# Expert-choice layers of a MetaFormer kernel: token statistics by VectorE, scales spread through DRAM, the eight largest found chunk by chunk

## The chip, the cores and the metric

The kernel runs on one core of a Trainium2 chip. The core has TensorE (PE: matrix multiplications and transposes, its weight loads are listed as PEld), VectorE (DVE), ScalarE (ACT), GpSimd (POOL) and SyncE (SP), which here only issues DMAs. Each engine works through its own instructions in order and waits on semaphores for the others. The metric is the device time of one execution in microseconds; lower is better.

## The reference, cut to what matters

A MetaFormer of four layers on an input of 4 images, 128 channels, 64 x 64 pixels. Each layer adds a token mixer and then a feed-forward part to `x`. The change concerns the feed-forward part of layers 1 and 2, which is the same code: a mixture of experts in which each of 64 experts chooses its 8 tokens out of 4096.

```
t = tokens(x)                                     # [4, 4096, 128]
n = (t - mean(t)) / sqrt(var(t) + 1e-5)           # per token, over its 128 channels
logits = einsum('bsd,ed->bse', n, gate_w) + gate_b
probs  = softmax(logits, axis=1)                  # over the 4096 tokens of an image
topv, topi = top_k(probs per expert, 8)           # 8 tokens for each expert and image
gathered = n[topi]
pooled   = einsum('bked,bke->bed', gathered, topv)
h   = gelu([pooled, 1] @ weight1[e])              # 128 -> 512
out = [h, 1] @ weight2[e]                         # 512 -> 128
t   = t + scatter_add(topi, out * topv)
```

## The kernel before, in words

`xs` holds the whole state in SBUF, [128 channels, 4 images, 4096 tokens], all in float32. `expert_choice` (line 1246) runs twice, for layers 1 and 2. It works on two pairs of images (`PAIRS`): a pair's 2 x 64 experts fill the 128 partitions of `chosen[p]`, [128, 4096]. The 4096 tokens of an image are cut into 8 chunks of 512 (`CH`, `NCH`).

Inside each `manual_schedule(engines=ORDERED)` block the instructions of PE, ACT, DVE and POOL stay in the order in which the code issues them. SP isn't in that set; its DMAs are put in order by the framework's scheduler, which also makes all waits and lets a tile's buffer be used again when its last reader is done.

Before the first block the weights of the first four groups of experts are asked for (`weights`, 8 DMAs of 1 MB, `load`, line 1316). Then the first stage (lines 1326 to 1533) does the following, in the order written at its end:

- `stat` (1337) centres one chunk by a matmul with `cent` (`moe_pd`, 128x512), squares it on ACT, and `variances` sums four squares at a time over the channels by matmuls with `ewin` into `pv`. 16 chunks make a pair. `scales` takes the square root on ACT, `inverted` the reciprocal on DVE (128x512), and `turn_scales` turns the scales so that tokens lie on partitions.
- `logits` (1383) spreads a chunk's scales over the experts by a matmul with the constant `own` (`moe_rb`), multiplies the tokens with the centred gate (`moe_pl`), copies the first to SBUF on ACT, multiplies both on DVE, and adds the bias on ACT.
- `rows` (1411) transposes a chunk of one image (four 128x128 transposes into a PSUM bank with the tag `b`, of which there are 3), copies it to one of five `xt` tiles and appends the token's scale (so that a table row has 128 + 16 numbers); a DMA on SP's queue writes it to `tables[p]` in DRAM.
- `largest` (1426) searches the 4096 logits of each expert for the eight largest (`max`, `max_index`), makes table rows of their places, and the negated maximum.
- `exponentials` and `denominators` (1441, 1447) sum the softmax on ACT, a chunk at a time.
- `ask` (1452) fetches one chosen token per expert from the table, by an indirect DMA of POOL; eight of them make a pair.
- `pool` (1462) multiplies `ident` with share and scale (`diag`) on DVE, and sums the eight gathered tokens by matmuls; a matmul with `cent` centres the sum, and a copy on DVE puts it into `pooled`.

The order: statistics of pair 0, five chunks of statistics of pair 1, logits and `largest` of pair 0, the rest of the statistics mixed with `rows` of image 0, logits of pair 1 mixed with `rows` and with exponentials of pair 0, `largest(1)`, the last `rows` and the `ask`s of pair 0, exponentials and `ask`s of pair 1, `pool(0)`, `pool(1)`.

The second stage runs the 16 groups of experts through `first`, `turn`, `second` and `hand`, with the weights coming from DRAM; the last stage multiplies each token's results back and adds them to `xs`.

Two other phases use forms that matter below: the recurrence of layer 0 measures its inputs with `bn_stats` (line 499), and the attention of layer 3 has an `inverse_root` of small VectorE operations (1853) and spreads its scales through DRAM (`spread` at 1922, `way` at 1925).

Of the kernel before, what the change touches and what calls it, by code (L numbers as in the profile page):

```python
# [17 lines left out]
F32 = mybir.dt.float32  # L18
# [1227 lines left out]
def expert_choice(net, layer):  # L1246
# [20 lines left out]
    K, ROW = 8, P + 16  # L1267
# [3 lines left out]
    with ExitStack() as ctx:  # L1271
        dram = ctx.enter_context(tc.tile_pool(name="moe_dram", bufs=1, space=bass.MemoryType.DRAM))
        tables = [dram.tile([2 * N, ROW], F32, name=f"moe_table{p}") for p in range(PAIRS)]
# [24 lines left out]
        behind = keep.tile([P, 1], F32, name="moe_behind")  # L1298
        nc.gpsimd.memset(behind[0:E], 0.0)
        nc.gpsimd.memset(behind[E:P], float(N))  # L1300
# [25 lines left out]
        with (  # L1326
# [5 lines left out]
            def bank(tag, name):  # L1332
                return ps.tile([P, CH], F32, name=f"moe_{name}", tag=tag, bufs={"a": 3, "b": 3}.get(tag, 1))

            stats = {}

            def stat(p, j):

                if j == 0:
                    stats[p] = (bank("pv", "pv"), [])  # L1340
                pv, squares = stats[p]
                pd = bank("a", "pd")
                nc.tensor.matmul(pd, net.cent, net.chunk(2 * p + j // NCH, j % NCH), start=True, stop=True)
                sq = sb.tile([P, CH], F32, name="moe_sq", tag="moe_sq", bufs=5)
                nc.scalar.activation(sq, pd, AF.Square)
                squares.append(sq)
                if j % 4 == 1 and j > 4:
                    variances(p, j // 4 - 1)

            def variances(p, r):  # L1350
                pv, squares = stats[p]
                for q in range(4):
                    nc.tensor.matmul(
                        pv[32 * q : 32 * q + 32],
                        net.ewin[:, 31 - r : 63 - r],
                        squares[4 * r + q],
                        start=r == 0,
                        stop=r == 3,
                    )

            rstds, turned = {}, {}

            def scales(p):
                variances(p, 3)
                rstd = sb.tile([P, CH], F32, name="moe_rstd", tag="moe_rstd")
                nc.scalar.activation(rstd, stats[p][0], AF.Sqrt, bias=net.eps[1e-5])
                rstds[p] = rstd

            def inverted(p):
                nc.vector.reciprocal(rstds[p], rstds[p])  # L1370

            def turn_scales(p):

                pt = bank("a", "pr")
                for k in range(4):
                    nc.tensor.transpose(pt[:, k * P : (k + 1) * P], rstds[p][:, k * P : (k + 1) * P], net.ident)
                turned[p] = sb.tile([P, 2, NCH, 4], F32, name="moe_turned", tag="moe_turned")
                nc.vector.tensor_copy(
                    turned[p].rearrange("p i (a q) k -> p k q (i a)", q=4),
                    pt.rearrange("p (k q r) -> p k q r", q=4, r=32)[:, :, :, 0:4],  # L1380
                )

            def logits(p, c):
                pb, pl = bank("b", "rb"), bank("a", "pl")
                q = c % 4
                rows = slice(32 * q, 32 * q + 32)
                nc.tensor.matmul(pb, own[rows, c // 4, :], rstds[p][rows], start=True, stop=True)
                for i in range(2):
                    nc.tensor.matmul(
                        pl[i * E : (i + 1) * E], cgate, net.chunk(2 * p + i, c), start=True, stop=True  # L1390
                    )
                lg = chosen[p][:, c * CH : (c + 1) * CH]
                nc.scalar.copy(lg, pb)
                nc.vector.tensor_mul(lg, lg, pl)
                nc.scalar.activation(lg, lg, AF.Identity, bias=gbias)

            xts = [sb.tile([P, 4, ROW], F32, name=f"moe_xt{i}", bufs=1) for i in range(5)]
            for t in xts:
                nc.gpsimd.memset(t[:, :, P:ROW], 0.0)

            own = sb.tile([P, 2, 2 * E], F32, name="moe_own", bufs=1)
            for q in range(4):
                group = slice(32 * q, 32 * q + 32)
                for r in range(2):
                    for i in range(2):
                        at = 32 * q + 2 * i + r
                        nc.gpsimd.tensor_copy(
                            own[group, r, i * E : (i + 1) * E], net.ident[group, at : at + 1].to_broadcast([32, E])
                        )

            def rows(b, c):
# [3 lines left out]
                for t in range(4):  # L1415
                    tok = slice((4 * c + t) * P, (4 * c + t + 1) * P)
                    nc.tensor.transpose(pt[:, t * P : (t + 1) * P], net.xs[:, b, tok], net.ident)
# [34 lines left out]
            def ask(p, j):  # L1452
                if j == 0:
                    asked[p] = sb.tile([P, K, ROW], F32, name="moe_asked", tag="moe_asked")
# [31 lines left out]
            for j in range(2 * NCH):  # L1486
                stat(0, j)
# [1144 lines left out]
```

## Time and profile before

| | us |
|---|---|
| median of 3 runs | 6042.37 (6040.1 to 6043.02) |
| the profiled execution's own time | 6034.38 |
| its span, first to last instruction | 6032.6 |
| first stage of `expert_choice`, layer 1 | 2461.8 to 2584.5 |
| second stage, layer 1 | 2584.5 to 2664.5 |
| first stage, layer 2 | 2934.9 to 3054.8 |
| second stage, layer 2 | 3054.8 to 3130.3 |

Over the span PE is busy 5684.2 us (94%), DVE 4380.3 (73%), ACT 3365.4 (56%), POOL 2057.2 (34%). In the first stage of layer 2 (119.9 us) PE is busy 101.0 us, ACT 72.3, DVE 44.6, at a granted TensorE clock of 0.91.

A line of the timeline gives the start and the duration in us, the engine, the line of the source, the operation, output and inputs with their shapes, how often it was merged, and in brackets how long the engine had idled before and what ended that. `SPq` is SP's queue of DMAs: its time is that of the issue, not of the transfer.

### The profile page before, as it was taken

Reading aid. Unit: us, or ns where it says so; the run is one execution under the profiler, and the core shown is the slowest. Engines: PE = TensorE matmul, PEld = TensorE weight load, DVE = VectorE, ACT = ScalarE, POOL = GpSimd, SP = SyncE. Lnnn points to the kernel's source line nnn. Section 1 sums busy time; section 2 is a strip of 40 time slices with the busy share of each in tenths; the row PEclk is TensorE's granted clock in tenths of the full one; section 3 lists DMA queues with packets and bytes.
Section 4 is the critical chain, followed back from the end, with each engine's and each line's share of the span. In section 5 each row is a group of like instructions: output and inputs, shape, how many; then the busy total and the mean of one; then the engine's idle time right before and its main releaser. Section 6 shows DMA issues by size and latency. Waiting matters only on the chain. (4 is left out here: it accounts for less than half of the span.)

```text
span 6032.6 us, 97814 instructions
## 1 busy us (share of the span) xinstructions
PE 5684.2 (94%) x39896; PEld 2250.6 (37%) x39927; DVE 4380.3 (73%) x4783; ACT 3365.4 (56%) x4213; POOL 2057.2 (34%) x2015
## 2 busy tenths in 40 slices
PE   8999999889999988879979999999999999999799
PEld 2222222346667766433333222322232223222233
DVE  6888887456767676456446888888888888888666
ACT  4444444333323322521336888888888888999421
POOL 3898897027777777200010111111111111111000
PEclk9999999989999999979989999999999999999899
DMA  6434432057777777550274666656665666666200
GB/s 215 98 74 90 89 76 47 1 150 231 217 229 217 228 221 210 167 183 0 88 266 111 133 155 146 138 130 154 146 141 128 151 148 142 133 131 131 60 25 27
DMA packets 273274, 818.39 MB, mean 136 GB/s; under 512 B 42644, under 2 KB 100392, under 8 KB 226728
## 3 DMA queue, kind: packets, MB, share of 16 engines
q0 software_dynamic: 109568, 505.75, 35.2%
q1 hardware_dynamic: 163240, 306.20, 17.5%
q8 instruction: 320, 5.24, 0.4%
q14 instruction: 146, 1.20, 0.1%
HBM read 416.71 MB, written 93.13 MB: 85 GB/s over the span
## 5 line engine op out<-in xcount | busy, mean ns | idle before, releaser
L2035 ACT ACTIVATE att_ex<-att_sc,att_shift 128x1024 f32<-128x1024 f32 x2048 | 2141.8, 1111 | 281.3 <-PE att_sc L2031 165.1
L2066 DVE TENSOR_TENSOR att_dve<-att_dve,att_ex 128x2048 f32<-128x2048 f32 x704 | 1631.5, 2317 | 154.0 <-ACT att_ex L2035 129.2
L2031 PE MATMUL att_sc<-att_q,att_k 32*128 32x512 f32 x8192 | 1280.8, 640 | 0.0
L2047 PE MATMUL att_pv<-att_ex,att_vals 128*32 128x512 f32 x8192 | 1092.2, 605 | 0.0
L998 POOL DMA_INDIRECT dcn_g<-dcn_table,dcn_idx x896 | 851.3, 950 | 354.3 <-issue 150.8
L412 DVE SCALAR_TENSOR_TENSOR inv_prod<-inv_pk,bspan,inv_seen 128x512 f32<-128x512 f32 (+1 forms) x1120 | 774.5, 743 | 141.4 <-PE inv_pk L399 141.0
L410 POOL TENSOR_TENSOR inv_prod<-inv_seen,inv_prod 128x512 f32<-128x512 f32 (+1 forms) x672 | 837.5, 1273 | 95.2 <-ACT inv_prod L409 95.2
L2064 POOL DMA_DIRECT2D att_dma<-att_ex x224 | 192.5, 859 | 1965.1 <-ACT att_ex L2035 1738.6
L409 ACT ACTIVATE inv_prod<-inv_pk,bspan 128x512 f32<-128x512 f32 (+1 forms) x672 | 436.1, 682 | 504.9 <-PE inv_pk L399 493.7
L2031 PEld LDWEIGHTS att_sc<-att_q,att_k 32*128 32x128 f32 x8192 | 423.5, 183 | 656.5 <-issue 416.8
L1006 DVE TENSOR_TENSOR dcn_g<-dcn_g,dcn_near_w 128x1024 f32<-128x1024 f32 x448 | 538.9, 1214 | 164.9 <-DMA dcn_g<-dcn_table,dcn_idx 153.4
L399 PE MATMUL inv_pk<-inv_red,wtap 32*96 32x512 f32 (+1 forms) x3584 | 512.1, 637 | 7.3 <-DVE wtap L377 7.3
L1015 PE MATMUL dcn_pt<-ident,dcn_g 128*128 128x128 f32 x3584 | 472.9, 276 | 34.0 <-ACT dcn_st L1120 16.4
L1015 PEld LDWEIGHTS dcn_pt<-ident,dcn_g 128*128 128x128 f32 x3584 | 419.1, 142 | 206.9 <-issue 116.1
L421 PE MATMUL inv_out<-inv_prod,inv_fold 96*32 96x512 f32 (+1 forms) x3584 | 478.6, 606 | 8.5 <-DVE xs L429 8.5
L2047 PEld LDWEIGHTS att_pv<-att_ex,att_vals 128*32 128x32 f32 x8192 | 161.8, 108 | 752.2 <-issue 727.0
L399 PEld LDWEIGHTS inv_pk<-inv_red,wtap 32*96 32x96 f32 (+1 forms) x3584 | 131.9, 171 | 386.2 <-DVE inv_prod L412 362.5
L1034 ACT ACTIVATE dcn_fold<-dcn_pf,dcn_turn 128x256 f32<-128x256 f32 x128 | 60.2, 473 | 366.0 <-PE dcn_pf L1030 366.0
L1120 ACT COPY dcn_st<-dcn_pt 128x512 f32<-128x512 f32 x224 | 129.9, 580 | 241.0 <-PE dcn_pt L1015 241.0
L1127 PE MATMUL dcn_out<-dcn_st,dcn_wk 128*128 128x512 f32 x448 | 236.0, 609 | 25.0 <-DVE xs L1135 23.1
L2536 PE MATMUL top_po<-top_xg,top_we 128*128 128x512 f32 x512 | 233.3, 599 | 0.0
L1054 DVE TENSOR_TENSOR dcn_square<-dcn_hx,dcn_by 128x512 f32<-128x512 f32 x192 | 130.0, 677 | 115.4 <-PE dcn_by L1040 75.5
(442 smaller groups left out, 5358.1 us busy)
## 6 DMA issues: line engine op xcount, KB each, us to landing
att_dma<-att_ex POOLq DMA_DIRECT2D x224, 1024.0 KB, 7.0
inv_seen<-inv_image SPq DMA_DIRECT2D x256, 266.0 KB, 9.1
moe_w<-in_L_ffn_weight SPq DMA_DIRECT2D x64, 1024.0 KB, 14.2
att_dma<-att_ex SPq DMA_DIRECT2D x32, 1024.0 KB, 9.0
att_dve<-att_dma POOLq DMA_DIRECT2D x32, 1024.0 KB
moe_table<-moe_xt SPq DMA_DIRECT2D x64, 288.0 KB, 2.8
dcn_table<-dcn_xt SPq DMA_DIRECT2D x32, 512.0 KB, 4.8
dcn_g<-dcn_table,dcn_idx POOLq DMA_INDIRECT x896, 3.7
```

What stands on the lines that cost most here:

```text
L399: nc.tensor.matmul(pk[0:m], wtap[half][rg, i, blk], red[rg, h * CH : (h + 1) * CH], start=True, stop=True)
L409: nc.scalar.activation(prod[0:m, h], pk[0:m], AF.Identity, bias=by)
L410: nc.gpsimd.tensor_mul(of, view, of)
L412: nc.vector.scalar_tensor_tensor(out=of, in0=as_shape(pk[0:m], of), scalar=by, in1=view, op0=ALU.add, op1=ALU.mult)
L421: nc.tensor.matmul(po[CR * blk : CR * (blk + 1), h, :], fold[0:m], prod[0:m, h, :], start=unit == 0, stop=unit == UNITS - 1,)
L998: nc.gpsimd.indirect_dma_start(out=g[:, t, :], out_offset=None, in_=rows, in_offset=bass.IndirectOffsetOnAxis(ap=idx[:, Q4 * c + i + t, k ...
L1006: nc.vector.tensor_mul(near, near, by)
L1015: nc.tensor.matmul(pt[0][:, (i + t) * P : (i + t + 1) * P], near[:, t, q, :], net.ident, is_transpose=True, start=i + t + q == 0, stop=i + ...
L2031: nc.tensor.matmul(pes[h // 2][:, h % 2, :], ks[r, t * P : (t + 1) * P], q[r], start=True, stop=True)
L2035: nc.scalar.activation(ex[:, 2 * two : 2 * two + 2, :], pes[two], AF.Exp, bias=shifts[g][:, two : two + 1],)
L2047: nc.tensor.matmul(block["pv"][r], vals[:, t, r], ex[:, h, :], start=t == 0, stop=t == NT - 1)
L2066: nc.vector.tensor_add(block[who], block[who], ex)
```

## The change

Nothing outside `expert_choice` is touched. A table row now is the token alone (128 numbers), and token 4p + t of a chunk lies on partition p (the transposes take every fourth token), so that a partition writes four rows in one piece. `rows` no longer needs the scales and so comes first. The token's statistics are taken by DVE from the transposed chunk in PSUM: four `bn_stats` of 128 numbers each, which give count, mean and spread of the even and the odd channels (`halves`); `variance` joins the two halves. `scales` takes square root and reciprocal of all 64 values per partition of a pair, transposes them, writes them to DRAM (`spread`), and `way` reads 512 scales back for each chunk, repeated on 64 partitions for each image; three `by` buffers hold them. `logits` multiplies with that tile.

`largest_of` finds the eight largest and their places in each chunk as it comes; `largest` searches the 64 candidates of the eight chunks and then looks up the eight places by eight comparisons with a counter (`order`). The scales of the fetched tokens are no longer fetched: `pool` measures the fetched rows again, and takes the inverse root by `inverse_root` on DVE. The `b` banks are 4 instead of 3, the `diag` buffers 3 instead of 4. The order of the stage is new.

```diff
-            for j in range(2 * NCH):
-                stat(0, j)
-            scales(0)
-            inverted(0)
-            for j in range(5):
-                stat(1, j)
-            turn_scales(0)
...
+            def variance(halves, out, apart):
+                nc.vector.tensor_sub(apart, halves[..., 1], halves[..., 4])
+                nc.vector.tensor_mul(apart, apart, apart)
+                nc.vector.tensor_add(out, halves[..., 2], halves[..., 5])
+                nc.vector.scalar_tensor_tensor(
+                    out=out, in0=apart, scalar=P / 4.0, in1=out, op0=ALU.mult, op1=ALU.add
+                )
+                nc.vector.tensor_scalar(out, out, 1.0 / P, 1e-5, op0=ALU.mult, op1=ALU.add)
...
+            def rows(b, c):
+                p, i = divmod(b, 2)
+                pt = bank("b", "pt")
+                for t in range(4):
+                    nc.tensor.transpose(pt[:, t * P : (t + 1) * P], net.chunk(b, c)[:, t:CH:4], net.ident)
+                xt = xts[(b * NCH + c) % len(xts)]
+                nc.scalar.copy(xt, pt.rearrange("p (t d) -> p t d", d=P))
+                for t in range(4):
+                    nc.vector.bn_stats(halves[p][:, i, c, t, :], pt[:, t * P : (t + 1) * P])
+                first = i * N + c * CH
+                nc.sync.dma_start(tables[p][first : first + CH, :].rearrange("(p t) r -> p t r", t=4), xt)
...
             def scales(p):
...
+                variance(halves[p].rearrange("p i c t h -> p (i c t) h"), var, apart)
+                nc.scalar.activation(var, var, AF.Sqrt)
+                nc.vector.reciprocal(var, var)
                 pt = bank("a", "pr")
+                nc.tensor.transpose(pt[0 : 2 * NCH * 4, 0:P], var, net.ident)
+                lines = sb.tile([2 * NCH * 4, P], F32, name="moe_lines", tag="moe_lines", bufs=1)
+                nc.vector.tensor_copy(lines, pt[0 : 2 * NCH * 4, 0:P])
+                nc.sync.dma_start(spread[p].rearrange("i c (t q) -> (i c t) q", q=P), lines)
+                for c in range(2):
+                    way(p, c)
+
+            def way(p, c):
+                by = ways[p, c] = sb.tile([P, CH], F32, name="moe_by", tag="moe_by", bufs=3)
+                for i in range(2):
+                    nc.sync.dma_start(by[i * E : (i + 1) * E], spread[p][i, c : c + 1, :].to_broadcast([E, CH]))
...
+                by = ways.pop((p, c)).rearrange("p (t q) -> p q t", t=4)
+                nc.vector.tensor_mul(lg.rearrange("p (q t) -> p q t", t=4), by, pl.rearrange("p (q t) -> p q t", t=4))
                 nc.scalar.activation(lg, lg, AF.Identity, bias=gbias)
+                if c + 2 < NCH:
+                    way(p, c + 2)
...
+            def largest_of(p, c):
+                lg = chosen[p][:, c * CH : (c + 1) * CH]
+                nc.vector.max(out=peaks[p][:, c, :], in_=lg)
+                nc.vector.max_index(out=spots[p][:, c, :], in_max=peaks[p][:, c, :], in_values=lg)
...
+                nc.vector.tensor_scalar_mul(negs[p], top[:, 0:1], -1.0)
+                nc.vector.max_index(out=place, in_max=top, in_values=flat)
...
+                for j in range(K):
+                    nc.vector.scalar_tensor_tensor(
+                        out=found[:, j, :],
+                        in0=order,
+                        scalar=at[:, j : j + 1],
+                        in1=known.rearrange("p c k -> p (c k)"),
+                        op0=ALU.is_equal,
+                        op1=ALU.mult,
+                    )
+                nc.vector.tensor_reduce(row, found, AX.X, ALU.add)
...
+                for j in range(K):
+                    nc.vector.bn_stats(own[:, j, :], asked[p][:, j, :])
+                var, root, spare = (small[:, n] for n in range(3))
+                variance(own, var, spare)
+                inverse_root(root, var, spare, small[:, 3].bitcast(I32))
+                nc.vector.tensor_mul(shares[p], shares[p], root)
...
+            for b in range(2):
+                for c in range(NCH):
+                    rows(b, c)
             scales(0)
+            left = [(b, c) for b in range(2, B) for c in range(NCH)]
+            for _ in range(6):
+                rows(*left.pop(0))
             for c in range(NCH):
                 logits(0, c)
+                for _ in range(2):
+                    if left:
+                        rows(*left.pop(0))
+                        if not left:
+                            scales(1)
+                if c > 0:
+                    largest_of(0, c - 1)
+            largest_of(0, NCH - 1)
             largest(0)
             for c in range(NCH):
                 logits(1, c)
+                ask(0, c)
+                exponentials(0, c)
+                if c > 0:
+                    largest_of(1, c - 1)
             denominators(0)
+            largest_of(1, NCH - 1)
             largest(1)
+            for c in range(K):
+                ask(1, c)
                 exponentials(1, c)
             denominators(1)
             pool(0)
```

More of the change, by code (lines that the diff above doesn't have):

```diff
@@ L1332, in bank @@
             def bank(tag, name):
[L1333 to L1361, printed above, removed]
-            def scales(p):
[L1364 to L1367, printed above, removed]
@@ L1369, in inverted @@
-            def inverted(p):
-                nc.vector.reciprocal(rstds[p], rstds[p])
-            def turn_scales(p):
-                pt = bank("a", "pr")
[L1375 to L1381, printed above, removed]
+                return ps.tile([P, CH], F32, name=f"moe_{name}", tag=tag, bufs={"a": 3, "b": 4}.get(tag, 1))
@@ L1398, in expert_choice @@
[L1398 to L1409, printed above, removed]
@@ L1453, in ask @@
                 if j == 0:
[L1454 removed]
+                    asked[p] = sb.tile([P, K, P], F32, name="moe_asked", tag="moe_asked")
                 nc.gpsimd.indirect_dma_start(
```

106 lines of the change are left out of this document (44 added, 62 removed).

## The prediction

> **What bounds the kernel now.** The table of engines on the page says only that TensorE is busy 94% of the span, an average over stages with different limits; the change touches the first stage of `expert_choice`, which runs once in layer 1 (2461.8 to 2584.5 us) and once in layer 2 (2934.9 to 3054.8 us). I read the timeline of that stage, then the DMA view of its opening, then rows of other phases that already run the operations the change adds.
>
> The timeline of layer 1 (start, duration, engine, line, operation; in brackets the idle time before it and what ended it):
>
> ```profile
> 2461.78 7.34 PE L1343 MATMUL moe_pd<-xs,cent 128*128 128x512 f32 x12 [7.15 <-PEq L1182]
> 2470.69 3.37 SPq L1322 DMA_DIRECT2D moe_w<-in_L_ffn_weight  x1
> 2483.95 3.35 DVE L1370 RECIPROCAL moe_rstd<-moe_rstd 128x512 f32<-128x512 f32 x1 [28.65 <-ACT moe_rstd L1366]
> 2491.12 0.69 DVE L1394 TENSOR_TENSOR moe_chosen<-moe_chosen,moe_pl 128x512 f32<-128x512 f32 x1 [1.70 <-PE moe_pl L1389]
> ...
> 2555.80 4.43 DVE L1428 MAX8 moe_top<-moe_chosen 128x8 f32<-128x4096 f32 x1 [0.72 <-ACT moe_chosen L1395]
> 2560.34 4.42 DVE L1431 FIND_INDEX8 moe_place<-moe_top,moe_chosen 128x8 uint32<-128x4096 f32 x1
> 2571.31 0.16 DVE L1450 TENSOR_REDUCE moe_total<-moe_sums 128x1 f32<-128x8 f32 x1 [5.82 <-ACT moe_sq L1445]
> 2571.84 2.86 DVE L1469 TENSOR_SCALAR moe_diag<-ident,moe_share,moe_asked 128x128 f32<-128x128 f32 x8
> 2584.21 0.29 DVE L1482 COPY moe_pooled<-moe_pc 128x128 f32<-128x128 f32 x1 [2.51 <-PE moe_pc L1481]
> ```
>
> TensorE with ScalarE sets the statistics (VectorE has idled 28.65 us before the first reciprocal); the logits start at 2491.1 in layer 1 and at 2961.6 in layer 2. At the end VectorE leads: `largest(1)`, then ScalarE's exponentials, then the two `pool` calls, 13.2 us from 2571.31 to 2584.5.
>
> The DMA view of 2455 to 2495, 1 us to a number:
>
> ```profile
> GB/s 231 401 397 10 0 8 25 88 225 395 372 92 145 317 401 391 356 399 414 387 383 391 391 383 385 385 389 391 387 111 23 0 0 0 0 0 0 0 0 0
> ```
>
> The queue of SP carries 8 MB of expert weights at 388 GB/s, and empties at 2484.4; the same in layer 2 until 2961.4. One weight load took SP 3.37 us to issue, so the queue is full. Before, the first `moe_table` write goes out at 2509.8, long after.
>
> From the recurrence and attention, operations like the added ones:
>
> ```profile
> 1087.70 2.59 DVE L499 BATCH_NORM_STATS2 rnn_stats<-rnn_pd 128x6 f32<-128x512 f32 x4
> ...
> 3178.39 0.19 DVE L1859 TENSOR_TENSOR att_scale<-att_scale,att_turned 128x32 f32<-128x32 f32 x1
> 3178.62 0.18 DVE L1860 TENSOR_SCALAR att_scale<-att_scale 128x32 f32<-128x32 f32 x1
> 3179.92 0.34 SPq L1922 DMA_DIRECT2D att_spread<-att_scale  x1
> 3181.39 4.82 SPq L1927 DMA_DIRECT2D att_by<-att_spread  x3
> 3184.58 0.69 DVE L1938 TENSOR_TENSOR att_k<-att_by,att_sc 128x512 f32<-128x512 f32 x1 [4.72 <-DMA att_by<-att_spread]
> ```
>
> A chain of small VectorE operations steps every 0.22 us; a spread through DRAM takes 4.7 us from its write's issue to the first use (3179.92 to 3184.58).
>
> **The change, part by part.** D is the moment when the weights have drained.
>
> *Opening.* Removed are 64 `moe_pd` and 64 `moe_pv` matmuls, 32 squares, the square roots and two 3.35 us reciprocals. Instead `rows` comes first and each row ends in a table write on SP's queue, behind the 8 MB. Only five `xt` buffers and four `b` banks exist: rows 0 to 4 are copied, rows 5 to 8 transposed and measured, then PE, ACT and DVE wait. The queue serves in order by the trace (weight loads land 14.2 us after issue, 14.9 in layer 2, about five loads of 2.7 us deep). So the first table lands at D + 2.3 (0.7 us for 256 KB at 388 GB/s, and the 1.6 that remain of the shortest landing, 2.4 us for 288 KB), row 5's copy takes 0.6, row 9's four transposes 0.6: row 9's statistics start at D + 3.5. The first matmul also waits for `moe_gate` (issued 2462.7 and 2934.3, some 2.3 to 3 us); D hides it, else 2 to 4 us. The 80 POOL memsets (0.09 us, 7 us) are needed only at `largest`.
>
> *Statistics.* Four `bn_stats` of 128 per row. The 512-wide one lasts 0.698 and steps every 0.63 (2.59 less the last, over 3); at 1.04 us per 1000 elements (the 4096-wide against 512-wide rows) 384 elements less is 0.23. Bounds: 0.14 with no fixed cost, 0.30 with no overlap (the 128x128 copy from PSUM is 0.289). I take 0.23, the same operation: 0.95 a row with its wait. [...]
>
> *VectorE from D + 3.5 to the places of pair 1.* ACT's copies (0.58 a row, the 32 of 0.2 for the scales gone) and PE's transposes (0.55; 0.75 if the step of four in their loads costs what L1560's does) stay below it. The removed `rb` matmuls (1.1 a chunk) and their ACT copies (0.58) stood on the logits' path of 2.06 a chunk, which VectorE's 2.17 to 4.1 replaces. 23 rows x 0.95 = 21.9. Two `scales` with nothing in between: five operations of 64 (1.1), square root 0.5 with its handoffs, reciprocal of 64 0.5 (128 take 0.9), transpose and copy 1.1: 3.2 x 2 = 6.4. The spread of pair 0 is hidden by six rows (5.7 against 4.7 plus 0.4 for the second half); uncovered it costs 5.1. Logits 16 x 0.65 = 10.4 (the scale tile is read with a step of 128 elements; the convolution's step of two costs nothing, 0.68), bias on ACT beside them. The eight largest of a chunk: MAX8 of 4096 is 4.43, so 0.16 fixed and 0.69 at 512; with the load (0.09) and FIND_INDEX8 1.52; x 16 = 24.3 (bounds 1.2 to 1.8), against 17.9 before, of which layer 1 exposed only the second pair's 9. `largest` on 64: two short searches, casts, eight scalar operations of 64 at 0.30 (by the 8-wide 0.23), a reduce: 4.3 x 2 = 8.6. Waits on SP: `way(0, 7)` stands behind pair 1's spread and two `way`s that need buffers of chunks 5 and 6, 2.5; in pair 1's loop a `way` is asked only two chunks ahead (3.7 round trip, 2.4 a chunk instead of 2.17), 2.0; last bias 0.3: 4.8. Sum 76.4: places of pair 1 at D + 79.9, that is 2564.3 (before 2565.4) and 3041.3 (before 3035.6).
>
> *Gathers.* `ask(0)` starts at once and is hidden. `ask(1)`: 8 x 1.25 plus 2.6 landing, done by D + 92.9; DVE reaches pool 1 at D + 97, so it is hidden.
>
> *End.* `negs` is written first, so exponentials(1) start at D + 76.0; 8 x 0.9, 0.3 and the reduce bring D + 83.6. Then the pools. Before: 7.0 and 6.3 us (layer 1: 2571.31 to 2578.3 to 2584.5), 6.3 and 6.0 with asks waited off (layer 2). Each adds eight `bn_stats` (1.8), variance (1.1), inverse root 14 x 0.21 = 2.9, one multiply 0.2 and 0.2 for three `diag` buffers instead of four: 6.2. End: D + 83.6 + 7.0 + 6.3 + 12.4 = 2593.7, +9.2 us; layer 2 D + 83.6 + 6.3 + 6.0 + 12.4 = 3069.7, +14.9.
>
> The later stage keeps its order and its 32 MB; it moves along. Its fifth weight group is issued when the first stage frees its memory (2584.24); were that address free early, 2 MB at 388 GB/s, 5.4 us a layer, would be gained; no row shows it, so I take nothing.
>
> Sum: +24 us. The profiled execution took 6034.4 and would take 6058.5; the runs shown have a median 8 us above it, 6042.4, and the forecast is **6066**.
>
> **Rivals.**
> - *Table writes don't queue behind the weights* (not slower). If DMA engines served them between the loads, statistics would begin at 2467 and 2937.5 and the 32 rows run through: 12.3 and 18.8 us earlier than the forecast, 24 - 31 = -7, 6035, no change. Landings of 14 us speak against it; it decides from 6 us a layer on, tables landing before D - 4.
> - *Cheap pieces*: `bn_stats` at 0.14 (108 x 0.09 = 9.7 a layer) and searches at 1.2 (4.8): -29, 6037, no change. The fixed cost in the rows of 512 speaks against it.
> - *The spread starves*: attention's `way` lands in 5.5 us median when the queue is used, not 3.2. Then pair 1's chunks take 3.3 and `way(0, 7)` 2 more: +9 a layer, 6084.
> - *Dear pieces*: 0.30 and 1.8: 108 x 0.07 + 4.8 = 12.4 a layer, 6091.
> - *Stage two starts early*: -11, 6055.
>
> **How the numbers follow.** Forecast 0.42, no queueing 0.14, cheap 0.12, starved spread 0.15, dear 0.12, early stage two 0.05. A measurement of this kernel tells about 0.2%, 12 us, from no change. The two cases at 6035 to 6037 give most of "same" and, where both or one meets an early stage two, of "faster": faster 0.10, same 0.19, slower 0.71. The range takes in all priced cases, with 5 us below the lowest: 6030 to 6092; the likeliest case by itself 6052 to 6080.
>
> **What would show it.** Right: `moe_table` writes issued from about 2474 and none landed before 2484; a gap of some 10 us on DVE ending near D + 3.5; first logits near D + 19 to 20; `bn_stats` 0.23 apart; pair 1's places at D + 80; about 6 us more in each pool, DVE busy through it. Wrong: tables landing before D, DVE idle in the middle of the chunk loops waiting for `moe_by`, or `moe_w` issued before the last `moe_pooled`.

## The result and the profile after

The changed kernel takes 6074.82 us (median of 5 runs, 6067.61 to 6076.99), the kernel before 6040.59 us in the same comparison (5 runs, 6037.6 to 6043.02): a ratio of 1.0057, with a 95% interval of 1.0045 to 1.0068. It is slower by 34 us; the forecast was 6066 us.

The profiled execution of the changed kernel is the one that took 6074.82 us (span 6073.0). Its phases against those of before, in us, read from the timeline. The first stage runs from the cast of `dcn_flag` (layer 1) or the end of the last addition of `conv_po` (layer 2) to the end of the last copy to `moe_pooled`; the second ends with the last addition and multiplication of `moe_ot`. (The table ahead of the prediction counts layer 1 from its first matmul, 6.6 us after the flag, and ends the second stages 1.1 us earlier, where `moe_ot` begins.)

| | before | after |
|---|---|---|
| start of the cast of `dcn_flag` | 2455.2 | 2460.8 |
| first stage, layer 1 | 129.3 | 143.4 |
| second stage, layer 1 | 81.2 | 78.6 |
| third stage and convolution | 269.2 | 268.7 |
| first stage, layer 2 | 119.9 | 139.6 |
| second stage, layer 2 | 76.6 | 77.1 |

The two first stages cost 283.0 us and not 249.2, 33.8 us more, which is nearly the whole difference of the medians. The spans of the two profiled executions differ by 40.4 us: besides the first stages, the flag comes 5.6 us later, in code that the change doesn't touch, and 1.0 us lies elsewhere.

The timeline of VectorE in layer 1 of the changed kernel (start, duration, engine, line, operation; in brackets the idle time before it and what ended it):

```profile
2476.19 4.25 DVE L1362 BATCH_NORM_STATS2 moe_halves<-moe_pt 128x6 f32<-128x128 f32 x20 [15.27 <-ACT moe_xt L1360]
2492.79 8.86 DVE L1362 BATCH_NORM_STATS2 moe_halves<-moe_pt 128x6 f32<-128x128 f32 x44 [12.36 <-ACT moe_xt L1360]
...
2511.67 1.06 DVE L1395 TENSOR_TENSOR moe_chosen<-moe_by,moe_pl 128x512 f32<-128x512 f32 x1 [0.73 <-DMA moe_by<-moe_spread]
2513.99 1.68 DVE L1362 BATCH_NORM_STATS2 moe_halves<-moe_pt 128x6 f32<-128x128 f32 x8 [1.26 <-ACT moe_xt L1360]
...
2546.99 1.03 DVE L1395 TENSOR_TENSOR moe_chosen<-moe_by,moe_pl 128x512 f32<-128x512 f32 x1 [2.25 <-DMA moe_by<-moe_spread]
...
2577.52 0.17 DVE L1436 CAST moe_idx<-moe_row 128x8 int32<-128x8 f32 x1
2580.18 0.16 DVE L1449 TENSOR_REDUCE moe_total<-moe_sums 128x1 f32<-128x8 f32 x1 [2.49 <-ACT moe_sq L1444]
...
2580.58 1.64 DVE L1478 BATCH_NORM_STATS2 moe_own<-moe_asked 128x6 f32<-128x128 f32 x8
...
2603.88 0.29 DVE L1492 COPY moe_pooled<-moe_pc 128x128 f32<-128x128 f32 x1 [2.15 <-PE moe_pc L1491]
```

VectorE now leads from the first statistic to the end. After five rows (20 statistics) it stands still for 12.36 us; in layer 2 for longer:

```profile
2980.11 8.80 DVE L1362 BATCH_NORM_STATS2 moe_halves<-moe_pt 128x6 f32<-128x128 f32 x44 [21.28 <-ACT moe_xt L1360]
```

What it waits for is a copy on ScalarE, and that waits for a table write. ScalarE's and SP's lines of the same timeline, and the DMA view of 2455 to 2495 (the last line: issues, KB each, median us from issue to landing):

```profile
2478.93 0.58 ACT L1360 COPY moe_xt<-moe_pt 128x512 f32<-128x512 f32 x1 [0.21 <-PE moe_pt L1358]
2492.18 2.45 ACT L1360 COPY moe_xt<-moe_pt 128x512 f32<-128x512 f32 x4 [12.66 <-DMA moe_table<-moe_xt]
```

```profile
2477.30 2.51 SPq L1327 DMA_DIRECT2D moe_w<-in_L_ffn_weight  x1
2479.91 20.81 SPq L1364 DMA_DIRECT2D moe_table<-moe_xt  x16
```

```profile
moe_table<-moe_xt SPq DMA_DIRECT2D x9, 256.0 KB, 10.2
```

SP issues the last of the 8 MB of weights at 2477.3, then the table writes; the one whose landing the trace shows there lands 10.2 us after its issue, where later ones of this stage take 2.0 to 3.4. The sixth copy needs the first of the five `xt` buffers back.

In the whole first stage of layer 1 (one row: start and end, length, busy time of PE, PEld, DVE, ACT and POOL with the number of instructions, granted TensorE clock, DMA share, GB/s), before and after:

```profile
2455.00:2585.00 130.00, 103.70 (x402) 45.31 (x402) 44.95 (x63) 73.70 (x168) 18.18 (x34) 0.87 0.47 149
```

```profile
2461.00:2605.00 144.00, 57.02 (x236) 36.54 (x236) 91.32 (x323) 44.62 (x89) 19.86 (x101) 0.64 0.45 155
```

The change does what it says: TensorE's busy time falls from 104 to 57 us and ScalarE's from 74 to 45, VectorE's doubles from 45 to 91. With some 52 us of idle time VectorE's stage is longer than TensorE's was. TensorE is idle more, and its granted clock in this stage was 0.64 where it had been 0.87.

### The profile page after: what moved, and what is told of

Its sections match the earlier page's. It is cut to its first block, busy times and chain, and to the rows that moved or that the text cites. A ratio compares the mean times of both kernels' runs of the same rounds, so it can differ in the third digit from the quotient of the medians.

```text
span 6073.0 us, 97689 instructions
## 1 busy us (share of the span) xinstructions
PE 5595.0 (92%) x39564; PEld 2229.2 (37%) x39595; DVE 4472.1 (74%) x5305; ACT 3307.2 (54%) x4055; POOL 2057.7 (34%) x2129
## 5 line engine op out<-in xcount | busy, mean ns | idle before, releaser
L1015 PE MATMUL dcn_pt<-ident,dcn_g 128*128 128x128 f32 x3584 | 473.6, 276 | 37.9 <-ACT dcn_st L1120 13.8
L1120 ACT COPY dcn_st<-dcn_pt 128x512 f32<-128x512 f32 x224 | 129.9, 580 | 241.9 <-PE dcn_pt L1015 241.9
```

The costliest lines, as they stand in the source:

```text
L1015: nc.tensor.matmul(pt[0][:, (i + t) * P : (i + t + 1) * P], near[:, t, q, :], net.ident, is_transpose=True, start=i + t + q == 0, stop=i + ...
```

## The experiments

The experiments ran on several chips. The kernel before took 6039 us on one and 6247 to 6263 us on the others, so times are compared only as ratios to the kernel before on the same chip, and stages by their lengths in the trace. The last column is the sum of the two first stages. Each stage length is read from one profiled execution; the two of the kernel before differ by 1.6 us in that sum.

| run | ratio to before (95%) | first stage, layer 1 | layer 2 | sum |
|---|---|---|---|---|
| before, first profile | | 129.3 | 119.9 | 249.2 |
| before, on a chip of the experiments | | 130.2 | 120.6 | 250.8 |
| the change | 1.0057 (1.0045 to 1.0068) | 143.4 | 139.6 | 283.0 |
| weights asked for late | 1.0027 (1.0017 to 1.0037) | 136.7 | 127.4 | 264.1 |
| tokens in order | 1.0035 (1.0021 to 1.0048) | 140.0 | 135.1 | 275.1 |
| no statistics in the pooling | 1.0021 (1.0012 to 1.0031) | 134.5 | 129.4 | 263.9 |
| chunks' eight alone, shared buffer | 0.9998 (0.9989 to 1.0007) | 134.0 | 121.7 | 255.7 |
| weights issued by ScalarE | 1.0011 (1.0002 to 1.0020) | 133.1 | 123.7 | 256.8 |
| rows ahead of logits | 1.0058 (1.0044 to 1.0072) | 144.2 | 139.4 | 283.6 |
| four edits | 0.9991 (0.9982 to 1.0000) | 128.1 | 117.0 | 245.1 |
| and scales in place | 0.9976 (0.9965 to 0.9987) | 120.5 | 111.8 | 232.3 |
| order, rows, scales in place | 1.0048 (1.0032 to 1.0064) | 140.9 | 136.4 | 277.3 |
| chunks' eight alone, apart | 0.9996 (0.9987 to 1.0006) | 129.9 | 121.4 | 251.3 |
| all, scales in halves | 0.9946 (0.9934 to 0.9958) | 116.0 | 106.8 | 222.8 |

**The weights late.** The theory is the prediction's first step: the table writes queue behind the weights.

```diff
-        weights = [load(g) for g in range(EARLY)]
+        weights = []
...
                 logits(1, c)
+                if c == 5:
+                    weights.extend(load(g) for g in range(EARLY))
                 ask(0, c)
```

> The changed kernel, with the four early weight groups (8 MB) asked for only after the last fetch of pair 1's scales, in the sixth chunk of pair 1, and not ahead of the stage. Theory (the table writes queue behind the weights, and through the five copy buffers hold up the statistics): the idle stretches of VectorE in the opening, 12.4 us in layer 1 and 21.3 us in layer 2 in the changed kernel's profile, go nearly whole, and the time falls by 25 to 33 us, to 6042 to 6050. Rival 1 (statistics, copies or transposes set the pace of the opening anyway): the wait is only renamed, and the time stays at 6070 to 6076. Rival 2 (8 MB in some 31 us asked for this late, behind which the gathered rows of pair 1 land late): the opening gains, and what it gains comes back at the end of the stage or in the first weight wait of stage two; 6055 to 6070.

The stages fell by 18.9 us and the ratio from 1.0057 to 1.0027 (6057 us for a kernel before of 6041): more than rival 1 allows, less than the theory, and in rival 2's range, but not by its mechanism. The reason is in SP's part of the timeline (layer 1):

```profile
2680.42 0.59 SPq L1325 DMA_DIRECT2D moe_w<-in_L_ffn_weight  x1
2684.53 11.66 SPq L1364 DMA_DIRECT2D moe_table<-moe_xt  x16
2696.24 0.45 SPq L1327 DMA_DIRECT2D moe_w<-in_L_ffn_weight  x1
```

SP's order isn't the code's: the scheduler had put three of the eight loads ahead of the first table write and the rest between the later DMAs. VectorE's lines show the two sides:

```profile
2684.53 12.95 DVE L1362 BATCH_NORM_STATS2 moe_halves<-moe_pt 128x6 f32<-128x128 f32 x64 [15.67 <-ACT moe_xt L1360]
...
2711.53 0.89 DVE L1362 BATCH_NORM_STATS2 moe_halves<-moe_pt 128x6 f32<-128x128 f32 x4 [5.68 <-ACT moe_xt L1360]
```

The 64 statistics of pair 0 run in one piece, 12.95 us; a wait of 5.68 us comes back later, behind the loads now put there. So the loads were next issued by ScalarE, whose order is fixed:

```diff
+                if c % 2 == 0:
+                    weights.append((load_first(c // 2, nc.scalar),))
+                else:
+                    weights[-1] += (load_second(c // 2, nc.scalar),)
                 if c > 0:
                     largest_of(1, c - 1)
```

> The changed kernel with the eight early weight loads issued by ScalarE, one for each chunk of pair 1, where its order is fixed (SyncE's is chosen by the scheduler, which in the run with late weights put three of the eight loads ahead of the first table write all the same). Theory (the table writes queue behind the weights): no idle stretch of VectorE over 2 us is left in the opening; against the changed kernel's 143.4 us the first stage of layer 1 is 10 to 14 us shorter, and against 139.6 us that of layer 2 is 17 to 23 us shorter; the time is 1.001 to 1.002 of the kernel before's. Rival 1 (the loads then collide with the fetches of pair 1's scales and with the gathers): half of that or less, ratio 1.003 or more. Rival 2 (the issues on ScalarE hold up the exponentials of pair 0 and with them the bias that the search waits for): the opening is free, and pair 1's chunks take 3 us and not 2.33.

The stages fell by 26.2 us, 10.3 in layer 1 and 15.9 in layer 2, and the ratio to 1.0011. From VectorE's list of waits in layer 1 (what waited, for what: us, times, longest):

```profile
DVE moe_halves L1370 <- DMA moe_b<-in_L_ffn_weight: 10.6, 1, 10.6
DVE moe_chosen L1403 <- DMA moe_by<-moe_spread: 8.8, 4, 3.4
DVE moe_halves L1370 <- ACT moe_xt L1368: 7.5, 6, 1.3
```

(The first row is the wait before the stage's first statistic, which the kernel after has too, 15.27 us long, with loads of weights ahead of the gate's DMA.) No wait for a copy is over 1.3 us: that the table writes waited behind the weights is shown, and it cost 26 us net, over three quarters of the 33.8. Whether they waited because they share SP's queue or because they share the DMA engines with the weights, this run doesn't separate, since it moves the loads in time as well. The gain is a little under what was expected, and rival 1 has a part in that: VectorE now waits longer for fetches of the scales, 8.8 us in layer 1 and 6.3 in layer 2 where the changed kernel had 3.0 and 2.9. Of the fetches of layer 1 whose landing the trace shows, two issued ahead of the first load land after 2.7 and 3.1 us, two issued behind it after 7.7 and 6.9, although the loads are on another queue. Rival 2 falls: where no fetch is late, pair 1's chunks still follow one another every 2.3 us.

**Tokens in order.** In the changed kernel the logits' multiply takes 1.02 us where the multiply before took 0.69. The scale tile is the only new operand, and it is read with a step of 128 numbers.

```diff
-                    nc.tensor.transpose(pt[:, t * P : (t + 1) * P], net.chunk(b, c)[:, t:CH:4], net.ident)
+                    nc.tensor.transpose(pt[:, t * P : (t + 1) * P], net.chunk(b, c)[:, t * P : (t + 1) * P], net.ident)
...
-                by = ways.pop((p, c)).rearrange("p (t q) -> p q t", t=4)
-                nc.vector.tensor_mul(lg.rearrange("p (q t) -> p q t", t=4), by, pl.rearrange("p (q t) -> p q t", t=4))
+                nc.vector.tensor_mul(lg, ways.pop((p, c)), pl)
```

> The changed kernel with each transpose taking 128 neighbouring tokens, as the kernel before did, so that the scales come back in token order and the logits' multiply reads them without a step (the table rows are then written in runs of 512 bytes). Theory (the step is what made the multiply 1.03 us where the kernel before had 0.69): 16 multiplies by 0.34 us less in each layer, on the engine that sets the pace: 5.4 us a layer, 11 in all, 6062 to 6066. Rival 1 (the step costs nothing, the multiply is long because its second operand comes from another place): the multiplies stay at 1.0 us and the time at 6072 to 6077. Rival 2 (runs of 512 bytes make the table writes late): the multiplies fall to 0.69 but the copies wait for the writes, 6070 to 6080.

The tile view of `moe_chosen` (duration in ns, least, median and most), the changed kernel first:

```profile
L1395 DVE TENSOR_TENSOR moe_chosen<-moe_by,moe_pl x16: 1004/1024/1058, 2511.7 to 2569.9; 128x512 f32<-128x512 f32 x16
```

```profile
L1394 DVE TENSOR_TENSOR moe_chosen<-moe_by,moe_pl x16: 667/669/689, 2738.4 to 2792.3; 128x512 f32<-128x512 f32 x16
```

The step cost 0.355 us a multiply, 5.7 us a layer. The two stages fell by 7.9 us together and the ratio by 0.0022. The rest of the 11.4 us went into idle time, most of it in layer 1, where VectorE idles 54.8 us instead of 52.5: one multiply waits 1.4 us, by the profile for a table write, and the copies of rows are waited for 1.0 us longer. The waits for fetches did not grow (2.5 us for one, where two had taken 3.0). Rival 1 falls: the operand still comes from the same place.

**No statistics in the pooling.**

```diff
-                for j in range(K):
-                    nc.vector.bn_stats(own[:, j, :], asked[p][:, j, :])
-                var, root, spare = (small[:, n] for n in range(3))
-                variance(own, var, spare)
-                inverse_root(root, var, spare, small[:, 3].bitcast(I32))
-                nc.vector.tensor_mul(shares[p], shares[p], root)
```

> The changed kernel without the statistics and the inverse root of the gathered rows: the shares go into the diagonals unscaled, so the pooled tokens lack each row's norm scale. Theory (nothing covers these operations, they stand in a row on VectorE between the reduce and the diagonals): 5.8 us in each of two poolings, 11.6 us a layer, 23 in all: 6050 to 6053. Rival (the gathered rows of pair 1 or the diagonals' banks come late anyway): only pair 0's half is won, 6061 to 6065.

The stages fell by 8.9 and 10.2 us, 19.1 together, the ratio to 1.0021. That is nearer the theory (23) than the rival (half): the operations stand in the path of both pairs, and a part returns as waits for TensorE between the two poolings (1.1 us ahead of the copy to `moe_b1t`).

**The chunks' eight alone.** The kernel before got this one part of the change.

```diff
             for c in range(NCH):
                 logits(1, c)
+                if c > 0:
+                    largest_of(1, c - 1)
```

> The kernel before with one part of the change alone: the eight largest from each chunk's eight, and the negated maximum taken first; the table rows are 136 wide and not 144, to make room. Theory (in the kernel before ScalarE sets the pace there: its copies of the last image's rows run to 2564.5 in the profile, the exponentials start at 2565.5 when VectorE has the maximum): VectorE has the maximum some 8 us sooner, but ScalarE is free only 1 us sooner, so 1 to 2 us a layer are won: 6036 to 6040. Rival 1 (VectorE's search sets the end of the stage): 7 to 8 us a layer, 6024 to 6028. Rival 2 (eight more searches a pair hold up the logits' loop): slower than before, 6042 to 6055.

The ratio is 0.9998, no difference, but the stage of layer 1 was 134.0 us. One suspect in the trace: `found` in `largest` takes a buffer that the squares of the statistics take turns in, and a square waited 2.25 us for it. So the part was tried again with `found` in a PSUM bank of its own:

```diff
-                found = sb.tile([P, CH], F32, name="moe_sq", tag="moe_sq", bufs=5)
+                found = bank("acc", "acc")
```

> The kernel before with the eight largest from each chunk's eight alone, as in the run of this part alone, but with the looked-up places in a PSUM bank of their own, and not in a buffer that the squares of pair 1's statistics take turns in: in that run a square waited 2.3 us for it, TensorE then stood still and worked at a lower granted clock (0.84 and 0.82 where the kernel before has 0.91 and 1.00). Theory (that stall ate the gain, and ScalarE sets the end as said): the stages are 1 to 2 us shorter each than in the kernel before, 250.8 us together on this chip: 247 to 249, ratio 0.9992 to 0.9998. Rival (the searches themselves delay the logits' multiplies): 252 us or more, ratio above 1.0003.

The ratio is 0.9996 and the stages take 251.3 us, 250.8 in the kernel before: the first run's 134.0 us in layer 1 are gone (129.9), and nothing is won. The buffer doesn't explain the 134.0: a square waited as long for it in layer 2, whose stage was as long as in this run (121.7 against 121.4), and in layer 1 the 4 us arise later. The eight multiplies of pair 1 start within 28.0 us there and within 24.7 here, at these granted clocks (the last column but two) in 15 us of that stretch, the shared buffer first:

```profile
2757.60:2772.60 15.00, 15.00 (x43) 6.36 (x42) 4.81 (x10) 9.43 (x25) 0.00 (x0) 0.58 0.32 94
```

```profile
2744.20:2759.20 15.00, 14.06 (x62) 6.32 (x61) 6.55 (x14) 12.21 (x32) 0.00 (x0) 0.96 0.41 122
```

The kernel before, which has no such sharing, took 24.6 us at a clock of 0.99 in its first profile and 26.6 at 0.80 in its second. So a single profile's stage can be some us longer at a lower clock; what lowered the clock, no run shows. VectorE and ScalarE at the end of layer 1's first stage:

```profile
2772.01 0.15 DVE L1443 TENSOR_SCALAR moe_neg<-moe_top 128x1 f32<-128x1 f32 x1
...
2785.39 0.16 DVE L1478 TENSOR_REDUCE moe_total<-moe_sums 128x1 f32<-128x8 f32 x1 [8.90 <-ACT moe_sq L1473]
```

```profile
2773.80 0.58 ACT L1423 COPY moe_xt<-moe_pt 128x512 f32<-128x512 f32 x1 [2.01 <-issue]
...
2779.62 0.72 ACT L1473 ACTIVATE moe_sq<-moe_chosen,moe_neg 128x512 f32<-128x512 f32 x1
```

The negated maximum is there at 2772.0, but ScalarE copies rows until 2779.6: VectorE's gain became a wait of 8.90 us. The searches of the whole tile had been hidden by ScalarE's copies.

**Rows ahead of logits.** Five times in each layer VectorE waits 1.26 us for a copy that stands behind the logits' bias on ScalarE.

```diff
-                logits(0, c)
                 for _ in range(2):
                     if left:
                         rows(*left.pop(0))
                         if not left:
                             scales(1)
+                logits(0, c)
```

> The changed kernel with the two rows of a chunk issued ahead of its logits, and not after them, in the loop of pair 0. Theory (in five chunks of each layer VectorE waits 1.26 us for a copy on ScalarE that stands behind the logits' bias): the five waits go, 6.3 us a layer, 12.6 in all; the ratio to the kernel before falls from 1.0057 to 1.0035 or so. Rival (the transposes or the bias are then late by as much): the waits go to another instruction, ratio 1.005 to 1.006.

The rival is right: 283.6 us against 283.0, ratio 1.0058. Four of the five waits are gone; in their place two fetches of scales are late and the first matmul of pair 1. From the list of waits in layer 1, rows ahead first, then the changed kernel:

```profile
DVE moe_chosen L1395 <- DMA moe_by<-moe_spread: 4.7, 2, 2.4
...
DVE moe_chosen L1395 <- PE moe_pl L1390: 1.6, 1, 1.6
```

```profile
DVE moe_chosen L1395 <- DMA moe_by<-moe_spread: 3.0, 2, 2.3
...
DVE moe_chosen L1395 <- PE moe_pl L1390: 0.2, 1, 0.2
```

and in layer 1 VectorE waits 1.0 us longer for the copies behind the table writes in the opening and 1.7 us more among the six rows.

**All together, and the fetches.** The four edits in one kernel (weights by ScalarE, tokens in order, rows ahead, and `pool` split so that pair 0's rows are measured and its diagonals made ahead of pair 1's sum, pair 1's measured while TensorE works):

```diff
-            denominators(1)
-            pool(0)
+            measure(0)
+            mix(0)
+            denominators(1)
+            measure(1)
+            finish(0)
```

> The changed kernel with these four at once: the weights issued by ScalarE, tokens in order, rows ahead of logits, and in the pooling the order changed (pair 0's rows are measured and its diagonals made ahead of pair 1's sum of exponentials, for which VectorE waited 2.5 us, and pair 1's rows are measured while TensorE works for pair 0). If the costs found are separate terms they add up: 14 + 21 (weights) + 9.5 (tokens in order, as measured) + 12 (rows) + 8 (pooling) = 64 us of the two first stages, 283 us in the changed kernel's profile and 249 in that of the kernel before: 219 to 230 us, and a ratio to the kernel before of 0.995 to 0.997. Rival (TensorE or the table writes set the pace once VectorE is quicker; the opening then waits for the transposes, and the pooling for the gathers): 235 to 250 us and a ratio of 0.998 to 1.000.

245.1 us, a gain of 37.9 of the 64 expected, ratio 0.9991: the rival's range. The first line of the list of waits in layer 1 names what came next:

```profile
DVE moe_chosen L1402 <- DMA moe_by<-moe_spread: 13.4, 6, 4.9
```

These waits are of two kinds. Before any weight load is issued, two multiplies of pair 0 wait 5.6 us together, where the fetches shown land 3.1 to 3.5 us after their issue: they are asked for late, two chunks ahead. Behind the first load four multiplies of pair 1 wait 7.8 us, and the fetches shown take 7.2 and 9.3 us. So the scales were fetched straight into the logits' own tile, which needs no turn of buffers:

```diff
-                by = ways[p, c] = sb.tile([P, CH], F32, name="moe_by", tag="moe_by", bufs=3)
+                by = chosen[p][:, c * CH : (c + 2) * CH].rearrange("p (c q) -> p c q", q=CH)
...
-                nc.vector.tensor_mul(lg, ways.pop((p, c)), pl)
+                nc.vector.tensor_mul(lg, lg, pl)
```

> The kernel with the four edits at once, and besides the scales fetched straight into the tile of the logits, two chunks a DMA, all of a pair's as soon as they are spread (no buffers of their own, so no fetch waits for an earlier multiply). Theory (once VectorE is quicker, the fetches two chunks ahead are what it waits for: 13.4 us in layer 1 and 10.0 us in layer 2 by the list of waits of the run with four edits): most of that goes, the two first stages fall from 245.1 to 222 to 230 us together, the ratio to the kernel before to 0.995 to 0.997. Rival 1 (2 MB of scales at once hold up the table writes behind them, and with these the copies): 235 to 242 us, ratio 0.997 to 0.999. Rival 2 (the weights in flight are what makes the fetches late, however early they are asked for): no change.

> The changed kernel with tokens in order, rows ahead of logits, and the scales fetched in place as in the last but without the weights' and the pooling's edits. Rows ahead alone won nothing, since the fetches of the scales and the transposes were late instead. Theory (the two limits stood one behind the other): now the rows' 12 us show, on top of 9.5 us for the order: the two first stages fall from 283 to 260 to 266 us, the ratio to 1.002 or 1.003. Rival (the waits move on once more, to the copies behind the table writes): 270 to 275 us, ratio 1.0035 to 1.0045.

With all edits: 232.3 us, ratio 0.9976, between the theory and rival 1, and both have a part. No multiply waits for its scales any more, but the eight fetches of 256 KB stand ahead of the row writes:

```profile
2692.73 4.99 SPq L1391 DMA_DIRECT2D moe_chosen<-moe_spread  x8
2697.82 22.45 SPq L1372 DMA_DIRECT2D moe_table<-moe_xt  x14
```

```profile
2705.66 0.89 DVE L1370 BATCH_NORM_STATS2 moe_halves<-moe_pt 128x6 f32<-128x128 f32 x4 [8.38 <-ACT moe_xt L1368]
```

Without the weights' and the pooling's edits the same wait (8.10 us) took all of the gain: 277.3 us against 275.1 for tokens in order alone. There the rival held, and by more than it priced (270 to 275 us). The last run treats that wait: half of a pair's scales are fetched at once, the other half after the first and the third chunk:

```diff
-                for c in range(0, NCH, 2):
+                for c in range(0, NCH // 2, 2):
                     way(p, c)
...
+                if c in (0, 2):
+                    way(p, c + 4)
```

> The kernel with all edits and the scales fetched in place, but half of a pair's scales at once and the other half after the first and the third chunk. With all at once, a copy of pair 1's rows then waited 8.4 us in layer 1 and 9.2 us in layer 2 behind a table write, 8 fetches (2 MB) having been put ahead of that write on SyncE's queue. Theory (small writes stand behind whatever is ahead of them in the queue): with 1 MB ahead the wait is 3 to 5 us, no multiply waits over 1 us for its scales, and the two first stages fall from 232.3 to 221 to 226 us; ratio 0.995 to 0.997. Rival (the wait is the write's own landing, not the queue): the wait stays at 8 to 9 us, the stages at 231 to 234, the ratio at 0.9975.

The wait fell to 4.12 us and the stages to 222.8 us, inside the theory's range; the ratio, 0.9946 (0.9934 to 0.9958), is better than it gave.

```profile
2703.35 0.89 DVE L1370 BATCH_NORM_STATS2 moe_halves<-moe_pt 128x6 f32<-128x128 f32 x4 [4.12 <-ACT moe_xt L1368]
```

This version is faster than both kernels: 0.54% below the kernel before and 1.1% below the change (1.0057 over 0.9946, on different chips).

**The kernel before on a chip of the experiments.**

> The kernel before, unchanged, profiled on the chip of these runs, since the kernel before took 6263 us on the chip of the first four runs and 6041 us on that of the first comparison. If the other chip is slower only in the deformable convolution's gathers (the granted clock and the instruction durations of the expert stage are alike), its first expert stage lasts 129 us in layer 1 and 120 us in layer 2, as in the first profile. If the whole chip is slower, these are 3 to 4% longer, and the comparison of stages across chips is off by some 5 us.

This was the chip of 6039 us, so it doesn't answer for the others; the stages are 130.2 and 120.6 us, within 1 us of the first profile. On the chips of 6247 us and more the kernel before was not profiled; that chunks' eight alone, apart, took 129.9 and 121.4 us on one of them speaks for stages of the same length.

## Why the prediction was right, and where it was not

Slower was right, and 6074.8 lies in the range; the two first stages cost 33.8 us more and not 24.1. The steps, in layer 1, with D, the moment when the weights have drained, moved by the flag's 5.6 us to 2490.0:

- *Opening: right, for its main part.* The first table landed before 2492.2, D + 2.2 (D + 2.3 predicted), and statistics went on at D + 2.8 (D + 3.5). The rival without queueing priced the queue at 31 us; taking the weights away gave 26.2. (The landing of 14.2 us that the prediction reads for layer 1 is the median of all weight loads whose landing the trace shows; none of them lies in layer 1's opening. The 14.9 of layer 2 does lie in its opening.)
- *"Rows 5 to 8 transposed and measured, then wait": wrong.* Only 20 statistics ran, those of the copied rows. VectorE measured each bank only after ScalarE had copied it: in both layers all eight waits for `moe_halves` name the copy (35.2 and 32.1 us), and each of the 32 rows' first statistic starts after its copy's end, by 0.03 us or more. What asks for that order, no run shows. I hadn't counted the second reader, so 27 rows were left and not 23.
- *Statistics at 0.95 a row: too dear.* 44 of them in 8.86 us are 0.20 us apart (0.28 each, overlapping), 0.81 a row. 27 x 0.81 = 21.9, the predicted 23 x 0.95 = 21.9: two errors cancel.
- *"Logits 16 x 0.65 = 10.4, the step costs nothing": wrong, and of the sum's own terms the furthest off.* 16 at a step of 0.96 are 15.4, 5.0 us more. I had taken the convolution's step of two numbers for a step of 128. Here a step of two cost nothing (0.68 us, where the multiply before took 0.69 without a step) and one of 128 cost 0.355 us.
- *"Bias on ACT beside them": wrong where rows stand between.* In five chunks the next row's copy stands behind the bias, and the bias behind the multiply: 5 x 1.26 = 6.3 us that the sum lacks. That ScalarE is busy only 44.62 of 144 us doesn't say that its next instruction is ready. (Taking four of the five waits away won nothing by itself: the time came back in other waits.)
- *Searches: cheaper than priced.* 1.39 us each and not 1.52, 22.3 against 24.3; `largest` 3.9 and 3.8 against 4.3 each. The scales took 4.1 and 2.9 us against 3.2 each; waits for fetches and TensorE 3.4 against 4.8, of which the foreseen one for `way(0, 7)` is 2.25 (2.5). The 9 us of search that the prediction calls exposed in layer 1 of the kernel before were not: taking them off VectorE's path won nothing there (chunks' eight alone, apart).
- *The sum to the places of pair 1:* 21.9 (statistics) + 7.0 (scales) + 15.4 (logits) + 22.3 (searches) + 7.7 (`largest`) + 3.4 (waits) + 6.3 (copies behind the bias) = 84.0 from D + 2.8, so D + 86.8; the trace has D + 87.7, the prediction D + 79.9. The first logits came at D + 21.7 (D + 19 to 20).
- *End: right.* From the reduce to the last copy 24.0 us, predicted 25.7; the two poolings grew by 5.5 and 5.3 us, predicted 6.2 each. The gathers were hidden, no `moe_w` came before the last `moe_pooled`, and the second stages changed by -2.6 and +0.5 us. (Three small sums of the prediction are off without bearing on the forecast: the gathers add up to D + 92.5 and not D + 92.9, and the bounds of the searches lie 5.1 and 4.5 us from the middle and not 4.8 on both sides.)

So the mechanism was right and the sum 10 us short: 5.0 us (the step) and 6.3 us (copies behind the bias) a layer were missed, and some 6 us a layer came back from pieces priced too high and the wait after the places (2.5 against 3.7 us). That the statistics came out at the predicted 21.9 us, with both factors off, was luck. The rival of the starved spread didn't decide here, but it is what the edits ran into.

## What to carry to other kernels

Before a small DMA that something waits for, count the bytes that are asked for ahead of it (behind the 8 MB of weights a table write landed 10.2 us after its issue, later ones after 2.0 to 3.4). In a queue that a scheduler orders, moving the line of code need not move the issue (three of eight loads stayed ahead in layer 1); issuing it from an engine whose order is fixed did (ScalarE: the two stages fell by 26.2 us). But another queue didn't take the loads out of the way of what came behind them: the fetches of scales then landed after 7 to 9 us and not 3. Work moved to an idle engine cost its busy time here (VectorE's rose from 45 to 91 us in layer 1) and also the waits of a longer chain between engines (6.3 us a layer for copies behind the bias): list, for each instruction in the loop, what stands ahead of its producer. A wait taken away can uncover the next one behind it, so single edits may show nothing (rows ahead of logits: 0 us alone) and still be needed (222.8 us with the rest).

## What was not expected of the hardware

The chips differ by 3.4 to 3.7% with the same kernel, and by what the traces show not in the expert stage. The first layers run alike (the recurrence's flag at 1085 to 1090 us), but the deformable convolution of layer 1 ends some 200 to 230 us later. From the groups of instructions (busy us, mean ns, then idle us before them), the changed kernel where the kernel before takes 6041 us, then the run with late weights where it takes 6263 us:

```profile
L998 POOL DMA_INDIRECT dcn_g<-dcn_table,dcn_idx x896 | 851.4, 950 | 354.2 <-issue 155.3
```

```profile
L998 POOL DMA_INDIRECT dcn_g<-dcn_table,dcn_idx x896 | 850.2, 949 | 562.2 <-issue 201.8
```

Each gather takes GpSimd as long to issue, but it idles 208 us more between them. Why, no run here shows.
